# Candidate products of five of eight time stretches moved into the recurrences of a four-layer stack

## The chip, the cores and the metric

The kernel runs on one core of one Trainium2 chip. The metric is the time of one execution in microseconds (us), device time, as the median of several runs. Engines are named as in the profile: PE is TensorE (matmuls; PEld its weight loads), DVE is VectorE, ACT is ScalarE, POOL is GpSimd, SP the queue that issues the DMAs.

## The reference

32 rows of 256 time steps and 256 features go through four residual layers:

```
x = x + L0(cond, x)   # gated recurrence: z, r = sigmoid(x W + h U + cond C + b), hh = tanh(x W + (r*h) U + ..)
x = x + L1(cond, x)   # h = tanh(h*leak + sigmoid(h Wh + x Wz + b) * x)
x = x + L2(x, cond)   # f, i = sigmoid(x W_f + b_f), sigmoid(x W_i + b_i); s = f + i + eps
                      # new = i / s * (x W_h + b_h)               <- "candidate", weighed by i
                      # cumulative sum of log(f / s), exponentials, cumulative sum of scaled new, plus cond's part
x = x + L3(x, cond)   # per row two adapted 256x256 matrices: x + gelu(x M1) M2
```

L0 and L1 are recurrences over time, one step after the other; L2 and L3 are not.

## The kernel before, in words

The work has two stages.

**The recurrences.** One loop runs over t = 0 to 256; step t does step t of L0 and step t-1 of L1, with all 32 rows in one go, four quadrants of PE side by side. In each step the program order is: the products of r and z from the last h (`w_U_rz`, in the helper `product`, L606), the sigmoids, then whatever is due in this step (below), L1's product of its input (`w_l_Wz`), r*h (L760) turned to rhT, the product `w_U_h`, the kept part (1-z)h (L764), L1's product `w_l_Wh`, tanh (L690), the scan that makes h (L672, in two halves, inputs `other` and `keep`), its turn to hT (L682), the addition of x and hT on POOL (L787), and the next step's input product `w_W_rzh`. On POOL the residual addition of step t-3 (L722) comes first in a step, behind r*h by a dependency set by hand. Two of every four steps (t%4 = 0 or 3) open a new PSUM bank for L0 with four bf16 matmuls (L633), and every eighth step (t%8 = 2) opens one for L1, of 512 columns, after the input product.

Work of the later layers is laid beside the steps by dictionaries from step to calls (`transfers`, `products`, `moves`, `additions`, `sums`, `sigmoids`), filled by hand-written plans. Two jobs of the adaptation come first: the weights of L3 (16 of the steps 5 to 36 hold a matmul of it and POOL additions of 128x128, L467) and the matrices of L3 (32 steps to t = 227, whose sums with the base matrices, L522, run on DVE in five cuts). L2's gates for the first six of eight stretches of 32 time steps (NW_H = 6) take the steps that are left: a unit is one stretch, eight rows (q) and one of two feature halves (e). A product of a unit is two matmuls (k = 0, 1) of 128x256 into one half of the PSUM tile `pg`; one matmul goes into a step, whole (L93), or, in a few of the last steps, both go into one step in four quadrants each (L115). Then ACT's sigmoid (L130), on DVE the sum f+i (L135, reads two tiles in SBUF) and the guard (s times eps plus f, L138), and three stores to DRAM (L143).

**The last layers.** They work on eight groups of four rows. An order written out by hand, HEAD once and then TURN for turn = 2 to 9, says which piece of which group comes when; each word names a stage and a place, and the same order holds for every engine's own instructions. Here are the stages that matter: `in` fetches g, s and i of a group from DRAM; `lf` makes the gates of the last two stretches; `ls`, `lg` their sum and guard on DVE; `c` the candidate, W_h times x, two matmuls of 512 columns over all eight stretches (2 rows, one feature half), four of them a group; `m` (weigh, L875) adds the bias to it and multiplies it by i, on DVE from PSUM; `ln` and `exp` on ACT; `sum` (L897), `w` (L903), `new` (L915), `cum` (L920) and `h0` (L924) on DVE; `x` (L931) adds the hidden state to the rows on POOL, by a dependency behind the DVE piece that precedes it in the list; `mid` and `last` are the two products of L3 (L938), with gelu on ACT between; `y` (L960) is the final addition on DVE, from PSUM. Of the DVE pieces only m and y read PSUM; the others with two tensor inputs read both from SBUF.

Of the kernel before, what the change touches and what calls it, by code (L numbers as in the profile page):

```python
# [16 lines left out]
B = 32  # L17
T = 256
# [11 lines left out]
CB = 8  # L30
NH = T // CT
NW_H = 6
EPS = 1e-8


# [4 lines left out]
def kernel(ctx: ExitStack, tc: tile.TileContext, a, out: bass.AP):  # L40
# [26 lines left out]
    def vec(name, c):  # L67
        i = VECS.index(name)
        return vecs[:, i, c : c + 1]
# [21 lines left out]
    def gate_product(ps, w, e, k, rows, h0, h1):  # L91

        nc.tensor.matmul(  # L93
            ps[:, 0 : (h1 - h0) * (rows.stop - rows.start) * CT].rearrange(
                "p (h b t) -> p h b t", h=h1 - h0, t=CT
            ),
            w[:, k, e * P : (e + 1) * P],
            X2[:, k, rows, h0 * CT : h1 * CT].rearrange("p b (h t) -> p h b t", t=CT),
            start=(k == 0),
            stop=(k == NC - 1),  # L100
        )

    def gate_unit(h, q, e, banks):

        t = {}

        def multiply(name, w, k, by_quadrants):
            rows = slice(q * CB, (q + 1) * CB)
            if not by_quadrants:
                gate_product(banks[name], w, e, k, rows, h, h + 1)  # L110
                return

            for j in range(Q):
                js = slice(j * SQ, (j + 1) * SQ)
                nc.tensor.matmul(  # L115
                    banks[name][js].rearrange("p (b t) -> p b t", t=CT),
                    w[:, k, e * P + js.start : e * P + js.stop],
                    X2[:, k, rows, h * CT : (h + 1) * CT],
                    start=(k == 0),
                    stop=(k == NC - 1),  # L120
                    skip_group_check=True,
                    tile_position=(0, j * SQ),
                )

        def unit_tile(name):
            t[name] = gu.tile([P, CB * CT], FP, name=f"gate_{name}", tag=f"gate_{name}")
            return t[name]

        def sigmoid(name):
            nc.scalar.activation(  # L130
                unit_tile(name), banks[name], AF.Sigmoid, bias=vec("b_" + name, e)
            )

        def add_up():
            nc.vector.tensor_add(unit_tile("s"), t["f"], t["i"])  # L135

        def guard():
            nc.vector.scalar_tensor_tensor(  # L138
                unit_tile("g"), t["s"], EPS, t["f"], ALU.mult, ALU.add
            )  # L140

        def store(name):
            nc.sync.dma_start(out=waiting[q][:, "gsi".index(name), e, h], in_=t[name])  # L143

        return multiply, sigmoid, add_up, guard, store

    parts_f = {}

# [19 lines left out]
    gi = ctx.enter_context(tc.tile_pool(name="gates_in", bufs=1))  # L168
    gated = {}

    def fetch_chunk(g, i, e, hs=slice(0, NW_H)):
        name = "gsi"[i]
        if e == hs.start == 0:
            pool, bufs = (gp, 2) if i == 2 and g % 3 else (gi, 1)
            gated[name, g] = pool.tile(
                [P, NC, NH, GB * CT], FP, name=f"in_{name}", tag=f"in_{name}", bufs=bufs
            )
        q, half = divmod(g, CB // GB)
        cols = slice(half * GB * CT, (half + 1) * GB * CT)
        nc.sync.dma_start(out=gated[name, g][:, e, hs], in_=waiting[q][:, i, e, hs, cols])  # L180

    def fetch(g, i):
        for e in range(NC):
# [16 lines left out]
    with ExitStack() as rec:  # L200
# [43 lines left out]
        def at(when, t, f, *args):  # L244
            when.setdefault(t, []).append((f, args))
# [307 lines left out]

        free = [t for t in range(CT + 3, T) if t not in products]
        twice = range(T - 14, T - 4, 2)
        free = sorted(free + list(twice))
        stored = {}
        for h in range(NW_H):  # L560
            for q in range(B // CB):
                for e in range(NC):
                    while free[0] < (h + 1) * CT + 3:
                        free.pop(0)
                    multiply, sigmoid, add_up, guard, store = gate_unit(
                        h, q, e, {"f": pg[:, 0], "i": pg[:, 1]}
                    )
                    for name, w in (("f", w_f), ("i", w_i)):
                        ts, free[:NC] = free[:NC], []
                        for k, t in enumerate(ts):  # L570
                            by_quadrants = any(t in twice for t in ts)
                            at(products, t, multiply, name, w, k, by_quadrants)
                        at(sigmoids, t, sigmoid, name)
                    at(sums, t + 1, add_up)
                    at(sums, t + 2, guard)
                    for n, name in enumerate("isg"):
                        stored[q] = t + 2 + n // 2 + (n == 2)
                        at(transfers, stored[q], store, name)
        first_late = [
            first_late_gate(name, w, e, {"f": pg[:, 0], "i": pg[:, 1]})  # L580
            for e in range(NC) for name, w in (("f", w_f), ("i", w_i))
# [16 lines left out]
        def due(when, t):  # L598
            return [f(*args) for f, args in when.get(t, ())]

        def product(ps, cols, hT, w):


            for k in range(NC):
                for j in range(Q):
                    last = nc.tensor.matmul(  # L606
                        ps[j * B : (j + 1) * B, cols],
                        hT[:, k, :],
                        w[:, k, j, :],
                        start=False,  # L610
                        stop=False,
                        skip_group_check=True,
                        tile_position=(0, j * B),
                    )
            return last
# [93 lines left out]
        with tc.manual_schedule():  # L709
# [16 lines left out]
            for t in range(T + 1):  # L726
# [15 lines left out]
                    finish_1()  # L742
                    late = None
                due(moves, t)
                due(products, t)
                if t == T:
                    first_late[1][1]()
                if run1:
                    if s == 0:
                        begin_1(0, U1_0)  # L750
                    done = product(p_1[s], cols_1(s), by_chunk(pairs1[s][:, :, 0]), w_1z)
                    if run0:

                        after(done, z_done)
                rh_done = kept_done = None
                if run0 and t > 0:
                    rh = sp.tile([P, S], FP, name="rh", tag="rh")
                    for c in range(NC):
                        cs = bass.ts(c, B)
                        rh_done = nc.vector.tensor_mul(rh[:, cs], r[:, cs], h[:, cs])  # L760
                    rhT = turned("rhT", rh)
                    product(p_0[t], cols_0(t, 2, 2), rhT, w_uh)

                    kept_done = nc.vector.scalar_tensor_tensor(  # L764
                        kept, z, 1.0, h, ALU.subtract, ALU.mult, reverse0=True
                    )

                    after(kept_done, rz_done)
# [82 lines left out]
        )  # L851

    def late(g, name, e):
        return gated[name, g][:, e, LATE].rearrange("p h n -> p (h n)")

    def late_sum(g, e):
        return nc.vector.tensor_add(late(g, "s", e), parts_f[g, e], late(g, "i", e))
# [3 lines left out]
            late(g, "g", e), late(g, "s", e), EPS, parts_f.pop((g, e)), ALU.mult, ALU.add  # L861
        )

    def candidate(g, u):
        r, e = divmod(u, NC)
        b0 = g * GB + r * 2
        ps = pp.tile([P, 512], FP, name="ps_c", tag="ps_c")
        pcs[g, u] = ps.rearrange("p (h n) -> p h n", h=NH)
        for k in range(NC):
            gate_product(ps, w_n, e, k, slice(b0, b0 + 2), 0, NH)  # L870

    def weigh(g, u):
        r, e = divmod(u, NC)
        m = gated["i", g][:, e, :, r * 2 * CT : (r + 1) * 2 * CT]
        return nc.vector.scalar_tensor_tensor(  # L875
            m, pcs.pop((g, u)), vec("b_c", e), m, ALU.add, ALU.mult
        )

    def logs(g, q):
# [77 lines left out]
    def finish(g, b):  # L957
# [15 lines left out]
    }  # L973

    TURN = """
        lf:0 new:2 new:3 cum:2 sum:0.0 mid:1 in:2 mid:0 sum:1.0 cum:3 h0:2.0 lf:1 sum:0.1
        sum:3.1 last:1 sum:1.1 sum:3.0 w:1 exp:1 h0:3.1 h0:2.1 w:0 ls:0 h0:3.0 ls:1 c:0
        sum:2.0 w:3 lg:0 lg:1 x:2 m:0 y:1 x:3 exp:0 last:0 c:1 m:1 exp:3 c:3 y:0 mid:2 mid:3
        new:1 sum:2.1 new:0 w:2 cum:0 cum:1 c:2 h0:0.1 h0:0.0 exp:2 ln:1 h0:1.1 h0:1.0 ln:0
        last:2 x:1 m:3 last:3 y:2 in:1 x:0 m:2 in:0 y:3  # L980
    """

    HEAD = """
        in:2@2 lf:0@0 ls:0@0 lf:1@0 lg:0@0 c:2@0 c:1@0 ls:1@0 lg:1@0 ln:1@0 m:2@0 m:1@0
        sum:2.1@0 sum:2.0@0 c:0@0 ln:0@0 m:0@0 w:2@0 sum:3.1@0 sum:0.1@0 in:2@1 in:1@1
        sum:3.0@0 sum:0.0@0 sum:1.1@0 w:0@0 lf:0@1 lf:1@1 c:3@0 sum:1.0@0 ls:1@1 c:3@1 m:3@0
        exp:0@0 in:0@1 w:1@0 m:3@1 new:0@0 exp:1@0 lg:1@1 ls:0@1 new:1@0 w:3@0 exp:2@0
        cum:1@0 c:1@1 cum:0@0 h0:1.0@0 h0:0.0@0 exp:3@0 h0:1.1@0 lg:0@1 ln:1@1 x:1@0 ln:0@1
        c:2@1 m:1@1 c:0@1 h0:0.1@0 in:1@2 x:0@0 m:2@1 m:0@1 in:0@2
    """  # L990

    with tc.manual_schedule():
# [82 lines left out]
```

## Time and profile before

| what | us |
|---|---|
| time, median of 3 runs (950.96 to 952.18) | 951.61 |
| span of the profiled execution, first to last instruction | 950.9 |
| start, to the first h of the recurrence | about 15 |
| recurrences, steps 1 to 255 | 15 to 733 |
| last steps of L1 and start of the last layers | 733 to 739 |
| last layers | 739 to 951 |

For the profiled execution the span is what is given as its own time; the median of the timed runs lies 0.7 us above it, the shortest run 0.1. A row of the timeline gives start, duration, engine, line, operation, output<-input, shapes and a count; several instructions in a row are merged, and the duration is then from the first start to the last end. An fp32 matmul appears as two records. The time in brackets is how long the engine had been idle, and what ended that. The table of windows gives the busy time of each engine in a stretch, the granted clock of PE and the share of time in which the DMA engines were at work (1.00 and 0.73 are such shares).

### The profile page before, as it was taken

The numbers are of one execution on the slowest core, as the hardware profiler recorded it, in microseconds if no ns is written. First come the engines' busy times: TensorE is split into PE (matmuls) and PEld (weight loads), VectorE is DVE, ScalarE is ACT, GpSimd is POOL, SyncE is SP. The second block draws the span as 40 slices with busy tenths as digits, with TensorE's granted clock in tenths as the row PEclk, the third lists the DMA queues.
The fourth block names the chain that finished last, engine by engine and source line by source line (L and its number), as shares of the span: only waits on it lengthen the run. The fifth ranks groups of instructions, "written<-read, shape, count | busy, mean of one in ns | idle before, by whom it ended". The sixth has DMA issues, their size and how long they took to land.

```text
span 950.9 us, 55227 instructions
## 1 busy us (share of the span) xinstructions
PE 919.3 (97%) x22822; PEld 630.0 (66%) x22822; DVE 788.3 (83%) x3409; ACT 573.3 (60%) x2652; POOL 236.0 (25%) x594
## 2 busy tenths in 40 slices
PE   7999999999999999999999999999999799999978
PEld 4666666666666666666666666666676467777756
DVE  5777788888888888888888888888877899999995
ACT  3455555555555555555555555555555878889973
POOL 1233322222222222222222222222222012222222
PEclk9999999999999999999999999999999999999989
DMA  8345212222222222222222222341232457777643
GB/s 259 114 118 156 80 52 87 71 73 91 70 88 78 86 76 66 92 71 87 72 72 92 66 92 66 121 131 61 83 115 74 132 166 231 230 219 223 190 156 124
DMA packets 109726, 107.72 MB, mean 113 GB/s; under 512 B 9857, under 2 KB 96673, under 8 KB 109474
## 3 DMA queue, kind: packets, MB, share of 16 engines
q1 hardware_dynamic: 109474, 104.19, 35.2%
q8 instruction: 179, 2.93, 1.4%
q14 instruction: 73, 0.60, 0.2%
HBM read 59.06 MB, written 45.09 MB: 110 GB/s over the span
## 4 chain that ended last, share of the span: by engine, by line
PE 81%; DVE 11%; ACT 3%; issue 2%; DMA 1%; SPq 0%; POOL 0%; DVEq 0%; POOLq 0%; ACTq 0%
PE p L606 46%; PE ps_l L938 11%; PE pg L93 10%; PE ps_c L93 5%; DVE h L672 5%; PE p L633 3%; PE ps_g L93 2%; PE pw L510 2%; ACT other L690 2%; DVE hT L682 1%; ACT r L690 1%; DVE cc L897 1%; DMA w_W_rzh<-in_W_rzh_dram 1%; DVE rh L760 1%; DVE gate_g L138 1%
## 5 line engine op out<-in xcount | busy, mean ns | idle before, releaser
L606 PE MATMUL p<-w_W_rzh,xT 128*32 128x192 f32 x4096 | 213.8, 326 | 0.7 <-DMA w_W_rzh<-in_W_rzh_dram 0.7
L690 ACT ACTIVATE other<-p 128x32 f32<-128x32 f32 x512 | 74.3, 200 | 171.6 <-PE p L606 171.6
L672 DVE TENSOR_TENSOR_SCAN h<-other,keep 128x64 f32<-128x64 f32 x512 | 121.3, 279 | 66.3 <-ACT other L690 62.9
L606 PE MATMUL p<-w_U_rz,hT 128*32 128x128 f32 x4080 | 166.1, 279 | 6.4 <-issue 0.3
L787 POOL TENSOR_TENSOR pairs<-xT,hT 128x64 f32<-128x64 f32 x256 | 82.3, 322 | 327.1 <-DVE other L803 301.9
L690 ACT ACTIVATE r<-p 128x32 f32<-128x32 f32 x510 | 72.8, 195 | 149.9 <-PE p L606 149.9
L722 POOL TENSOR_TENSOR X<-pairs,h1T 128x64 f32<-128x64 f32 x256 | 102.7, 401 | 214.7 <-DVE rhT L682 211.1
L606 PEld LDWEIGHTS p<-w_U_rz,hT 128*32 128x32 f32 x4080 | 97.0, 108 | 85.8 <-DVE hT L682 83.7
L672 DVE TENSOR_TENSOR_SCAN pre<-other,pairs 128x128 f32<-128x128 f32 x256 | 123.4, 482 | 33.9 <-ACT pairs L794 0.2
L606 PEld LDWEIGHTS p<-w_W_rzh,xT 128*32 128x32 f32 x4096 | 124.4, 110 | 22.9 <-DMA w_W_rzh<-in_W_rzh_dram 1.4
L606 PEld LDWEIGHTS p<-w_l_Wz,pairs 128*32 128x32 f32 x4096 | 78.2, 110 | 84.7 <-issue 69.3
L794 ACT ACTIVATE pairs<-h1T,leak 128x32 f32<-128x32 f32 x510 | 133.6, 314 | 0.4
L606 PE MATMUL p<-w_l_Wz,pairs 128*32 128x64 f32 x4096 | 119.2, 225 | 3.5 <-ACT keep L740 0.9
L606 PE MATMUL p<-w_U_h,rhT 128*32 128x64 f32 x4080 | 106.2, 221 | 0.0
L606 PE MATMUL p<-w_l_Wh,h1T 128*32 128x64 f32 x4080 | 104.1, 219 | 0.0
L760 DVE TENSOR_TENSOR rh<-r,h 128x32 f32<-128x32 f32 x510 | 75.0, 189 | 32.2 <-ACT r L690 6.2
L682 DVE STREAM_TRANSPOSE hT<-h 128x32 f32<-128x32 f32 x512 | 84.2, 198 | 0.0
L931 POOL TENSOR_TENSOR X<-X,w 128x512 f32<-128x512 f32 x32 | 41.0, 1291 | 162.3 <-DVE in_g L860 99.5
L682 DVE STREAM_TRANSPOSE rhT<-rh 128x32 f32<-128x32 f32 x510 | 80.0, 195 | 0.0
L606 PEld LDWEIGHTS p<-w_l_Wh,h1T 128*32 128x32 f32 x4080 | 76.2, 110 | 0.1
L606 PEld LDWEIGHTS p<-w_U_h,rhT 128*32 128x32 f32 x4080 | 69.6, 108 | 5.0
L719 ACT ACTIVATE h1T<-pre 128x64 f32<-128x64 f32 x256 | 69.7, 272 | 1.1 <-DVE pre L672 1.1
(110 smaller groups left out, 1472.7 us busy)
## 6 DMA issues: line engine op xcount, KB each, us to landing
adapted<-wm SPq DMA_DIRECT2D x128, 128.0 KB
wt<-adapted SPq DMA_DIRECT2D x28, 512.0 KB
w<-in_W_dram SPq DMA_DIRECT2D x32, 256.0 KB
out_dram<-y SPq DMA_DIRECT2D x32, 256.0 KB
xT<-in_xT_dram SPq DMA_DIRECT2D x60, 128.0 KB
gates<-gate_i SPq DMA_DIRECT2D x48, 128.0 KB
gates<-gate_s SPq DMA_DIRECT2D x48, 128.0 KB
gates<-gate_g SPq DMA_DIRECT2D x48, 128.0 KB
```

What stands on the lines that cost most here:

```text
L93: nc.tensor.matmul(ps[:, 0 : (h1 - h0) * (rows.stop - rows.start) * CT].rearrange("p (h b t) -> p h b t", h=h1 - h0, t=CT), w[:, k, e * P ...
L606: last = nc.tensor.matmul(ps[j * B : (j + 1) * B, cols], hT[:, k, :], w[:, k, j, :], start=False, stop=False, skip_group_check=True, tile_ ...
L672: nc.vector.tensor_tensor_scan(*(x[:, ns].rearrange("p n u -> p (n u)") for x in (done, other, pairs)), 0.0, ALU.mult, ALU.add,)
L682: nc.vector.transpose(dst[:, c], src[:, bass.ts(c, B)])
L690: nc.scalar.activation(dst[:, bass.ts(c, B)], src[:, bass.ts(c, B)], function)
L719: nc.scalar.activation(flat(h1T), pre, AF.Tanh)
L722: return nc.gpsimd.tensor_add(X2[:, :, :, s], by_chunk(pairs1.pop(s)[:, :, 0]), h1s.pop(s))
L760: rh_done = nc.vector.tensor_mul(rh[:, cs], r[:, cs], h[:, cs])
L787: nc.gpsimd.tensor_add(by_chunk(pairs1[t][:, :, 0]), x_of(t), hT)
L794: nc.scalar.activation(by_chunk(pairs1[s][:, :, 1])[:, c], h1T[:, c], AF.Copy, scale=leak[:, c : c + 1],)
L931: after(nc.gpsimd.tensor_add(x, x, ws[g][:, b]), on_vector)
L938: nc.tensor.matmul(ps[:, e, :], matrices[row][:, m, k, e * P : (e + 1) * P], src[:, k, :], start=(k == 0), stop=(k == NC - 1),)
```

## The change

The change makes the candidate of the first five stretches (NC_H = 5) in the recurrences too. A unit there now has three products, f, i and c, for h < 5, and two for h = 5: 136 instead of 96, each of two matmuls. The products take the two halves of `pg` in turn. Where there are not enough free steps a step is "doubled": both matmuls go into it, by quadrants, and then L1's `w_l_Wz` is issued behind `w_U_h` instead of ahead of it, and the wait for z, which its last matmul took early, goes to the last quadrant matmul. 84 of the 188 steps that hold gate products are doubled. The sum f+i moves from DVE to POOL, with no dependency of its own behind other work of the step. A new DVE piece, `weigh_unit`, multiplies the candidate with i, in place, one step after its product, and the store of i follows that; the guard goes to a step that holds no weighing. The fetch of group 0 begins three steps later (t = 243 instead of 240), since the last store of its rows comes at t = 241 instead of 238.

In the last layers the candidate is left with three stretches: it now goes by four rows and 384 columns, two a group instead of four, and so does the weighing. HEAD and TURN are new. In TURN four `x` pieces stand as `h0:2.0 ls:0 x:2 new:3 sum:0.0`, `h0:3.1 exp:1 x:3 new:0 y:0 ls:1`, `h0:0.1 x:0 new:1 lg:0 w:2` and `h0:1.1 x:1 y:2 .. m:1 .. m:0 y:3` (other engines' pieces left out); before they stood as `lg:1 x:2 m:0 y:1 x:3 m:1 y:0` and `x:1 m:3 y:2 x:0 m:2 y:3`.

```diff
+NC_H = 5
...
-            nc.vector.tensor_add(unit_tile("s"), t["f"], t["i"])
+            nc.gpsimd.tensor_add(unit_tile("s"), t["f"], t["i"])
...
+        def weigh_unit(bank):
+            nc.vector.scalar_tensor_tensor(
+                t["i"], bank, vec("b_c", e), t["i"], ALU.add, ALU.mult
+            )
...
+        banks = pg[:, 0], pg[:, 1]
+        begins = {t for t in range(T) if t % 4 in (0, 3)}
+        free = [t for t in range(CT + 3, T - 1) if t not in products]
+        wanted = [
+            (h, q, e, name) for h in range(NW_H) for q in range(B // CB) for e in range(NC)
+            for name in ("f", "i", "c")[: 3 if h < NC_H else 2]
+        ]
...
+            while free[0] < max((h + 1) * CT + 3, last_read[n % 2]):
+                free.pop(0)
+            short = NC * (len(wanted) - n) - len(free)
+            now = free.pop(0)
+            if short > 0 and (now not in begins or short > sum(t not in begins for t in free)):
+                doubled.add(now)
+            for k in range(NC):
+                if k and now not in doubled:
+                    now = free.pop(0)
+                at(products, now, multiply, bank, w, k, now in doubled)
+            if name == "c":
+                at(sums, now + 1, weigh_unit, bank)
+                busy.add(now + 1)
+                last_read[n % 2] = now + 2
+                at(transfers, now + 2, store, "i")
...
+            at(sums, t + 1, add_up)
+            t += 2
+            while t in busy:
+                t += 1
+            busy.add(t)
+            at(sums, t, guard)
...
-                due(products, t)
+                multiplied = due(products, t)
...
-                    done = product(p_1[s], cols_1(s), by_chunk(pairs1[s][:, :, 0]), w_1z)
-                    if run0:
-
-                        after(done, z_done)
+                    if t in doubled:
+                        after(multiplied[-1], z_done)
+                    else:
+                        done = product(p_1[s], cols_1(s), by_chunk(pairs1[s][:, :, 0]), w_1z)
+                        if run0:
+
+                            after(done, z_done)
...
                     product(p_0[t], cols_0(t, 2, 2), rhT, w_uh)
+                    if t in doubled:
+                        product(p_1[s], cols_1(s), by_chunk(pairs1[s][:, :, 0]), w_1z)
...
+    def candidate(g, e):
         ps = pp.tile([P, 512], FP, name="ps_c", tag="ps_c")
...
+            gate_product(ps, w_n, e, k, slice(g * GB, (g + 1) * GB), NC_H, NH)
...
     TURN = """
+        new:2 lf:0 sum:3.1 lf:1 sum:2.0 mid:0 sum:3.0 cum:2 sum:1.0 c:1 sum:1.1 h0:2.1 h0:2.0
+        ls:0 x:2 new:3 sum:0.0 sum:0.1 cum:3 w:0 mid:1 h0:3.0 exp:0 w:1 h0:3.1 exp:1 x:3 last:0
+        last:1 new:0 mid:2 y:0 ls:1 cum:0 lg:1 sum:2.1 y:1 h0:0.0 in:2 h0:0.1 x:0 new:1 mid:3
+        lg:0 w:2 last:2 cum:1 w:3 exp:2 h0:1.0 last:3 ln:1 h0:1.1 x:1 y:2 ln:0 in:1 exp:3 m:1
+        c:0 m:0 y:3 in:0
     """
```

## The prediction

> **What bounds the kernel now.** I read the page first: TensorE (PE) is busy nearly all the span, VectorE (DVE) 83% of it, GpSimd (POOL) a quarter.
>
> ```profile
> PE 919.3 (97%) x22822; PEld 630.0 (66%) x22822; DVE 788.3 (83%) x3409; ACT 573.3 (60%) x2652; POOL 236.0 (25%) x594
> ```
>
> Such shares mix two stages. The timeline of the recurrences (to about 736 us) shows a fixed rhythm: `w_U_rz` starts at 665.32, 668.12, 670.92, so 2.80 us a step. Steps with a gate product keep that rhythm, and so do the few without one: the step is a chain (hT, `w_U_rz`, sigmoid, rh, turn, `w_U_h`, tanh, the h scan, turn), and the product lies in a gap of PE. What counts here is whether anything reaches the chain. One step, with the places that the change touches:
>
> ```profile
> 663.90 0.40 POOL L722 TENSOR_TENSOR X<-pairs,h1T 128x64 f32<-128x64 f32 x1 [0.82 <-DVE rhT L682]
> ...
> 664.03 0.36 DVE L522 TENSOR_TENSOR wm<-pw,w_base_upT 128x204 f32<-128x204 f32 x1
> ...
> 664.30 0.41 DVE L135 TENSOR_TENSOR gate_s<-gate_f,gate_i 128x256 f32<-128x256 f32 x1
> ...
> 664.69 0.48 DVE L672 TENSOR_TENSOR_SCAN h<-other,keep 128x64 f32<-128x64 f32 x2
> ```
>
> The sum f+i (L135) sits just ahead of the h scan and ends as it starts: no delay. POOL is free from 664.30 until hT is there.
>
> In the last layers I read the busy time of four turns of the list, each 24.35 us; one of them (columns: us, PE, PEld, DVE, ACT, POOL, clock, DMA share, GB/s):
>
> ```profile
> 824.56:848.91 24.35, 24.35 (x98) 18.10 (x97) 23.76 (x41) 21.75 (x32) 5.12 (x5) 1.00 0.73 226
> ```
>
> PE is full, DVE 0.6 us short of it. The change takes work from both, so DVE bounds next, and the third view asks what else holds DVE up. At the tail two POOL adds (L931) meet DVE:
>
> ```profile
> 921.47 1.29 DVE L960 TENSOR_TENSOR y<-ps_l,X 128x512 f32<-128x512 f32 x2
> ...
> 921.71 2.94 POOL L931 TENSOR_TENSOR X<-X,w 128x512 f32<-128x512 f32 x2 [11.36 <-DVE w L903]
> ...
> 922.67 0.85 DVE L915 TENSOR_TENSOR w<-in_i,w 128x512 f32<-128x512 f32 x1
> ...
> 923.44 1.75 DVE L897 TENSOR_TENSOR_SCAN cc<-f,s 128x256 f32<-128x256 f32 x1
> ```
>
> y, with one input in PSUM, runs beside POOL at its usual 0.69 each. L915, with two inputs in SBUF, takes 0.85 instead of 0.68; L897, also two, takes 1.75 instead of 0.67 and ends 0.54 after POOL does. POOL's pair takes 2.94 instead of 2.50: its second add stood still until L915 was through, then ran ahead of the scan. The same elsewhere: L924 at 759.48 takes 1.13 instead of 0.47 beside an L931, and L135 takes 0.55 (697.70) when L722 is still running, ending 0.28 after it. L522, L875 and L960, which read PSUM, never lengthen. So POOL and a DVE operation with two SBUF inputs exclude each other, and POOL goes next in turn. The old list puts its L931s beside y and m.
>
> **The change, part by part.** Times are against the profiled span, 950.9; the median of the runs is 951.61, 0.7 more.
>
> (1) *f+i moves to POOL, 48 times.* On POOL 128x128 (L467) takes 0.45 and 128x512 (L931) 1.28, so 128x256 by a straight line takes 0.73. It stands behind L722 in POOL's order, so it runs from about 664.27 to 665.00 of the step shown. The h scan has two SBUF inputs (other, keep) and starts at 664.69. A blocked scan ends its streaming after POOL: 0.28 after it for 128 columns (L672 pre beside L787), so about 0.145 for the 64 of one half. The first half then ends at 665.15 instead of 664.97: 0.17 on the chain (0.15 to 0.20 by where the add begins). 48 x 0.17 = **+8.2**. Bounds: nothing if the scan isn't held; 48 x 0.3 = 14.4 if it restarts whole. I take 0.17, since three kinds of DVE rows show that shape. Queued behind the add on POOL is L787, which waits for hT anyway, and behind L787 the next step's `w_l_Wz`. That the add also waits for the store of an older f+i is no news: L135 did too.
>
> (2) *40 candidate products (80 matmuls) join 96 gate products; 84 steps now hold both matmuls of a product, by quadrants.* In the old plan five such steps took 2.887, because `w_l_Wz` stood ahead of `w_U_h`. The new one puts it behind `w_U_h`, so rhT is met in time, but its 16 records, 0.225 from first to next (675.17 to 675.40 for their like), now stand ahead of the next `w_U_rz`. The wait for z goes from `w_l_Wz` to the last quadrant matmul; behind it waits `w_U_h`, which needs rhT 0.3 later anyway. What room is there? Here is a step that opens a new bank for layer 1 (t%8 = 2):
>
> ```profile
> 673.48 0.40 PE L633 MATMUL p<-parts,eye 128*32 128x512 bf16 x4
> ...
> 673.72 0.64 PE L606 MATMUL p<-w_U_rz,hT 128*32 128x128 f32 x16
> ```
>
> The 512 columns stream for about 0.21, to 673.69: room 0.03. Where layer 0's bank is opened (t%4 = 0 or 3), the last `w_W_rzh` matmul leaves about 0.06; in the others, without that 0.16, 0.22 to 0.24. I counted the plan: of 84 double steps 27 have t%8 = 2, 9 have t%4 = 0 or 3, 48 neither. 27 x 0.19 + 9 x 0.16 = 6.6. Nine of these 36 also carry a sum, whose delay gives PE the room: less 9 x 0.16 = 1.4. **+5.1**. The 48 others cost nothing, hidden by 0.22; if that is short by 0.05 they cost 2.4. Bounds: 0, if the modelled ends are late, to 36 x 0.225 + 2.4 = 10.5. The five old late steps go: **-0.4**.
>
> (3) *weigh* (128x256, one input in PSUM) takes the place on DVE that f+i leaves: L875 at 512 columns takes 0.745, less 256 columns at 1.04 ns = 0.48, against 0.41: at most 0.03 late in the 29 steps that also hold an L522, **+0.2**. The store of i follows it instead of the sigmoid; count and size of the stores stay, and SP's queue is idle for 2 us and more between issues there (701 to 733), which hides them; without that a late store would hold only the fetches at the start of the last layers. ACT's sigmoids are the same 96.
>
> (4) *Last layers, one turn.* PE loses 16 records of 0.43 and gains 8 of 0.32: 24.35 - 6.9 + 2.6 = 20.05. ACT has five table loads where it had six (1.28 each): 20.5. DVE loses 4 x 0.66 (L875, start to start) and gains 2 x 0.53: the rest sums to 20.9 by start-to-start rows, with 0.1 that I can't place: 22.05. So DVE would set a turn of 22.05, were there no POOL. But the new list sets x:2 ahead of new:3, sum:0.0; x:0 ahead of new:1, lg:0; x:3 ahead of new:0, y:0, ls:1; only x:1 lies beside y:2, m:1, m:0. By the tail rows each L931 lets one DVE operation through, then holds the next for 1.1 to 1.2: x:2 1.15, x:0 1.15, x:3 0.55 (y:0 fills half), x:1 0. Sum 2.85, turn **24.9**: 0.55 more than now. The fetches stay behind ln as now and land a few us later, ln of the next group 20 us later. The waits of DVE don't hide the 2.85: exp:0 ends 0.4 ahead of new:0, ln and exp:3 by two and more.
>
> (5) *Head and end.* DVE's head starts at 739.4 and sums start at 743.8, as now (ACT's table load and logarithms come first); then 14.1 of DVE work instead of 17.6, and the 2.2 and 1.0 waited for candidates go: new:2 at 758.4 instead of 764.1, -5.7. Turn 2 pays for x:0 and x:1 of group 0 as well, +2.2 + 0.55; turns 3 to 7 +0.55 each, 2.75; turn 8 (22.9 now; 24.9 - 2.4 without m, ls, lg) -0.4; the last turn, rows one by one instead of in pairs, 12.9 instead of 14.5, -1.6. Together **-2.2**. Bounds: 22.05 a turn gives -25; 1.2 for every x gives +6.
>
> Sum: 8.2 + 5.1 - 0.4 + 0.2 - 2.2 = +10.9: span 961.8, median run **962.5**.
>
> **Rivals.** *A, faster:* an L931 doesn't overtake a queued DVE operation but waits for the next that reads PSUM. Place: the last layers; price: the 2.85 a turn. Then turns are 22.05 (6 x -2.3), the head keeps its 5.7, turn 8 saves 3.2, the end 2.6: -25, and with +13 ahead of it 939. It decides once x costs under 1.2 a turn. For it: L960 runs beside every L931 now. Against: the scan at 923.44, overtaken. 0.20. *B, no price in the recurrences:* the add is done early enough and PE's modelled ends are late: 951.6 - 2.2 = 949.5. For it: halves of L467 beside the scan cost nothing. Against: those end at 47.23, the scan starts at 47.21; this add ends 0.3 later. 0.12. *C, a cold PE:* PE idles 4.9 us a turn, most of it ahead of mid:3, which waits for x:3. After 4.45 us of idleness at 759.62 a 512-column record took 0.85 instead of 0.43, for about 4 us; after 1.48 us (737.52) nothing happened. If each turn pays 2.4 for it and y waits: 6 x 2.4 = 14, 976. Against: last:2 has some 3 us to y:2. 0.10.
>
> [...]
>
> **The numbers.** My forecast 0.58, A 0.20, B 0.12, C 0.10. Forecast alone: 954 to 970, by its bounds. The range 941 to 974 leaves out half of A and half of C. What measurement can tell from no change is 0.2%, 1.9 us: faster 0.24 (A and a third of B), same 0.08, slower 0.68.
>
> **What would show it.** Right: in steps with a POOL sum the h scan takes 0.17 longer and the step 2.97; double steps at t%8 = 2 last 2.99, other double steps 2.80; in a turn, L897, L860 or L903 lengthen to 1.7 beside L931, and the turn is 24.9. Wrong: steps of 2.80 throughout, or turns near 22. A later last hT than 733 + 13 means a part of (1) or (2) is too small.

## The result, and the profile after

The changed kernel takes 968.64 us (median of 4 runs, 967.94 to 969.12) where the kernel before takes 951.89 in the same session: a ratio of 1.0172, with a 95% interval of 1.0156 to 1.0188. It is slower by 16.7 us; 10.9 had been forecast. The profiled execution spans 967.3 us, 16.4 more than before. The last h of the recurrences ends at 754.05 instead of 733.18, so the recurrences are 20.9 longer; the rest takes 213.3 instead of 217.7, 4.4 less.

Line numbers after the change: L606 (`product`) is now L638, L672 (scans) L704, L690 (tanh) and its like L722, L722 (residual) L754, L135 (f+i) L134, L897 (sum) L931, L903 (w) L937, L915 (new) L949, L920 (cum) L954, L924 (h0) L958, L931 (x) L965, L938 (products of L3) L972, L960 (y) L994; `ls` is L894 and `lg` L897 now, and L714 the turn (L682). The busy times:

```profile
PE 916.9 (95%) x23830; PEld 661.3 (68%) x23830; DVE 795.6 (82%) x3385; ACT 572.7 (59%) x2646; POOL 295.3 (31%) x642
```

PE has 1008 matmul records more and is yet 2.4 us less busy; POOL is busy 59 us more. DVE is busy 7 us more; a DVE operation that waits for POOL counts as busy (an L937 of 1.71 us below, where 0.68 is usual).

**A step with a sum.** Timeline of one step of the recurrences after the change (start, duration, engine, line, operation):

```profile
548.52 0.40 POOL L754 TENSOR_TENSOR X<-pairs,h1T 128x64 f32<-128x64 f32 x1 [0.84 <-DVE rhT L714]
...
548.88 0.72 POOL L134 TENSOR_TENSOR gate_s<-gate_f,gate_i 128x256 f32<-128x256 f32 x1
549.08 0.29 ACT L722 ACTIVATE other<-p 128x32 f32<-128x32 f32 x2 [0.68 <-PE p L638]
549.31 0.62 DVE L704 TENSOR_TENSOR_SCAN h<-other,keep 128x64 f32<-128x64 f32 x2 [0.58 <-ACT other L722]
```

The scan of h starts on time and takes 0.62 where it took 0.48; POOL's add runs until 549.60, into it. Over the trace a step of this kind lasts 2.955 (median of the six that have no doubled step beside them), a plain one 2.798: 0.156 more.

**A doubled step without a sum.** The same view, some 90 us earlier:

```profile
456.69 0.65 PE L638 MATMUL p<-w_U_rz,hT 128*32 128x128 f32 x16
...
457.33 1.15 PE L115 MATMUL pg<-X,w_W_i 128*32 128x256 f32 x16
...
457.58 0.24 ACT L772 ACTIVATE keep<-p 128x64 f32<-128x64 f32 x1
...
457.86 0.31 DVE L714 STREAM_TRANSPOSE rhT<-rh 128x32 f32<-128x32 f32 x2
...
458.22 0.43 PE L638 MATMUL p<-w_U_h,rhT 128*32 128x64 f32 x15
...
458.49 0.22 PE L638 MATMUL p<-w_U_h,rhT 128*32 128x64 f32 x1
...
458.75 0.29 ACT L722 ACTIVATE other<-p 128x32 f32<-128x32 f32 x2 [0.79 <-PE p L638]
```

From `w_U_rz` to tanh it is 2.06 here (456.69 to 458.75); in the step with the sum, which is not doubled, it was 1.94 (547.14 to 549.08). There `w_U_h` began 1.47 after `w_U_rz` and its sixteen records started within 0.19 (its row: 548.61, 0.41 long, the last record 0.22); here it begins at 1.53 (458.22), 0.22 after the last product record of the first quadrant (458.00), which is the pace at which that quadrant's records had started (457.33, 457.57, 457.79, 458.00), and the last record, in the quadrant whose matmuls waited for z (`keep`, to 457.82), starts 0.27 after the first. rhT is ready 1.48 after `w_U_rz` (at 458.17), as in plain steps, so the lateness arises behind it. From the end of one h to the end of the next, the median of the 59 doubled steps without a sum is 2.92: each is 0.12 late in itself, at any place of the eight-step pattern.

**A turn in the last layers.** DVE and POOL at x:0:

```profile
847.33 3.61 POOL L965 TENSOR_TENSOR X<-X,w 128x512 f32<-128x512 f32 x1 [3.85 <-DVE w L958]
```

```profile
847.11 0.68 DVE L949 TENSOR_TENSOR w<-in_i,w 128x512 f32<-128x512 f32 x1
847.72 0.41 DVE L897 SCALAR_TENSOR_TENSOR in_g<-in_s,gate_f 128x256 f32<-128x256 f32 x1
848.05 0.68 DVE L937 TENSOR_TENSOR w<-cc,s 128x512 f32<-128x512 f32 x1
848.65 1.21 DVE L954 TENSOR_TENSOR_SCAN w<-anew,w 128x512 f32<-128x512 f32 x1
849.79 1.71 DVE L937 TENSOR_TENSOR w<-cc,s 128x512 f32<-128x512 f32 x1
```

x:0 needs 1.28 alone and stands for 3.61: L949, under way, and three more (L897, L937, L954) run at their usual lengths, and only the fifth, L937, is held, for 1.03. The turn is 24.45 (x:0 to x:0, 847.33 to 871.79), and in it DVE has no gap while PE does (row of the table of windows):

```profile
850.00:875.00 25.00, 22.52 (x92) 18.05 (x91) 25.00 (x39) 21.01 (x31) 9.33 (x6) 0.93 0.74 230
```

### The profile page after: what moved, and what is told of

The parts are those of the page before. It is cut to its first block, busy times and chain, and to the rows that moved or that the text cites. A ratio compares the mean times of both kernels' runs of the same rounds, so it can differ in the third digit from the quotient of the medians.

```text
span 967.3 us, 57349 instructions
## 1 busy us (share of the span) xinstructions
PE 916.9 (95%) x23830; PEld 661.3 (68%) x23830; DVE 795.6 (82%) x3385; ACT 572.7 (59%) x2646; POOL 295.3 (31%) x642
## 3 DMA queue, kind: packets, MB, share of 16 engines
q8 instruction: 186, 3.05, 1.3%
## 4 chain that ended last, share of the span: by engine, by line
PE 74%; DVE 16%; ACT 4%; issue 3%; DMA 2%; POOL 0%; SPq 0%; POOLq 0%; DVEq 0%; ACTq 0%
PE p L638 49%; PE pg L115 9%; PE pg L94 7%; DVE cc L931 4%; PE p L665 3%; DVE h L704 2%; PE ps_l L972 2%; PE pw L517 2%; DVE w L958 1%; DVE w L949 1%; DVE w L954 1%; DVE w L937 1%; DVE y L994 1%; ACT other L722 1%; DMA in_i<-gates 1%
## 5 line engine op out<-in xcount | busy, mean ns | idle before, releaser
L638 PE MATMUL p<-w_W_rzh,xT 128*32 128x192 f32 x4096 | 226.6, 326 | 0.0
L704 DVE TENSOR_TENSOR_SCAN h<-other,keep 128x64 f32<-128x64 f32 x512 | 125.5, 286 | 78.7 <-ACT other L722 76.9
L722 ACT ACTIVATE other<-p 128x32 f32<-128x32 f32 x512 | 74.6, 199 | 182.2 <-PE p L638 182.2
L638 PE MATMUL p<-w_U_rz,hT 128*32 128x128 f32 x4080 | 169.5, 278 | 4.4 <-DVE hT L714 1.4
L754 POOL TENSOR_TENSOR X<-pairs,h1T 128x64 f32<-128x64 f32 x256 | 102.7, 401 | 221.7 <-DVE rhT L714 214.5
L722 ACT ACTIVATE r<-p 128x32 f32<-128x32 f32 x510 | 72.8, 195 | 138.8 <-PE p L638 134.9
L704 DVE TENSOR_TENSOR_SCAN pre<-other,pairs 128x128 f32<-128x128 f32 x256 | 123.3, 482 | 35.3 <-POOL pairs L824 1.3
L638 PEld LDWEIGHTS p<-w_W_rzh,xT 128*32 128x32 f32 x4096 | 135.6, 110 | 21.7 <-issue 2.1
L638 PEld LDWEIGHTS p<-w_U_rz,hT 128*32 128x32 f32 x4080 | 104.1, 108 | 67.1 <-DVE hT L714 65.1
L638 PE MATMUL p<-w_l_Wz,pairs 128*32 128x64 f32 x4096 | 127.8, 223 | 3.9 <-ACT keep L772 1.6
L638 PEld LDWEIGHTS p<-w_l_Wz,pairs 128*32 128x32 f32 x4096 | 89.7, 110 | 58.3 <-issue 45.6
L638 PE MATMUL p<-w_U_h,rhT 128*32 128x64 f32 x4080 | 118.7, 221 | 0.1
L638 PE MATMUL p<-w_l_Wh,h1T 128*32 128x64 f32 x4080 | 116.2, 219 | 0.7 <-issue 0.7
L965 POOL TENSOR_TENSOR X<-X,w 128x512 f32<-128x512 f32 x32 | 67.4, 2108 | 131.9 <-DVE w L958 94.6
L638 PEld LDWEIGHTS p<-w_U_h,rhT 128*32 128x32 f32 x4080 | 83.0, 108 | 14.8 <-DVE keep L801 0.3
L638 PEld LDWEIGHTS p<-w_l_Wh,h1T 128*32 128x32 f32 x4080 | 87.5, 110 | 1.2 <-issue 0.9
L714 DVE STREAM_TRANSPOSE hT<-h 128x32 f32<-128x32 f32 x512 | 84.1, 199 | 0.0
L972 PE MATMUL ps_l<-mid,wt 128*128 128x256 f32 x256 | 66.7, 419 | 14.9 <-ACT mid L985 14.9
L714 DVE STREAM_TRANSPOSE rhT<-rh 128x32 f32<-128x32 f32 x510 | 80.2, 195 | 0.0
```

The lines of the kernel that those rows point to most:

```text
L638: last = nc.tensor.matmul(ps[j * B : (j + 1) * B, cols], hT[:, k, :], w[:, k, j, :], start=False, stop=False, skip_group_check=True, tile_ ...
L704: nc.vector.tensor_tensor_scan(*(x[:, ns].rearrange("p n u -> p (n u)") for x in (done, other, pairs)), 0.0, ALU.mult, ALU.add,)
L714: nc.vector.transpose(dst[:, c], src[:, bass.ts(c, B)])
L722: nc.scalar.activation(dst[:, bass.ts(c, B)], src[:, bass.ts(c, B)], function)
L754: return nc.gpsimd.tensor_add(X2[:, :, :, s], by_chunk(pairs1.pop(s)[:, :, 0]), h1s.pop(s))
L965: after(nc.gpsimd.tensor_add(x, x, ws[g][:, b]), on_vector)
```

## The experiments

My theory after this: (a) the add on POOL holds the h scan; (b) a doubled step is late by its own quadrant matmuls and the wait for z on the last of them, and, where a bank is opened, makes the next step late by `w_l_Wz`; (c) DVE bounds the turn, and the new list puts `x` where it holds DVE up. The main rival for (a) and (b): the extra work on PE and DVE costs, wherever it stands. For (c): the clock, 0.93 in the row above, where PE idles 2.5 of 25 us.

A ratio is always to the kernel before, timed again in the same session, for its own median moved from session to session (951.89, 954.39, 952.24, 953.93 us). So runs are compared by their ratios; a difference of two of them is uncertain by about 0.003, some 3 us. Positions such as the last h come from one profiled execution of each run.

**f+i back on DVE.**

```diff
-            nc.gpsimd.tensor_add(unit_tile("s"), t["f"], t["i"])
+            nc.vector.tensor_add(unit_tile("s"), t["f"], t["i"])
```

> One part undone: the sum f+i is back on DVE, all else as in the changed kernel (968.6). Theory (the sum on POOL holds up the h scan, because both read two tiles in SBUF): in steps with a sum that are not doubled the 0.156 us go (23 of them), in doubled ones only about 0.04, because those are 0.117 late already and the end of the POOL sum hides that: -4.5 in all, 964. If the two prices add up without overlap: 48 x 0.156 = -7.5, 961. Rival (the new steps are late because DVE and PE are crowded, and where the sum runs doesn't matter): no change or slower, since DVE gets 0.41 us more in 48 steps: 968 to 972.

Measured: ratio 1.0131 (1.0107 to 1.0156), 0.0041 under the changed kernel, or 3.9 us. Its timeline at the same step:

```profile
547.23 0.56 DVE L134 TENSOR_TENSOR gate_s<-gate_f,gate_i 128x256 f32<-128x256 f32 x1
547.67 0.29 ACT L722 ACTIVATE other<-p 128x32 f32<-128x32 f32 x2 [0.68 <-PE p L638]
547.90 0.47 DVE L704 TENSOR_TENSOR_SCAN h<-other,keep 128x64 f32<-128x64 f32 x2
```

The sum now pays for its meeting with L754 (0.56 instead of 0.42) and still ends before the scan, which takes 0.47. Steps with a sum go from 2.955 to 2.808, doubled steps with a sum only from 2.958 to 2.919. So the two delays of one step don't add: the add on POOL ends at a fixed time, and a scan that is late by 0.12 anyway finds it 0.04 from done. 23 single steps x 0.147 + 25 doubled x 0.04 = 4.4. In the profiled execution itself the last h came just 1.2 earlier; other steps were longer there, of which more below. So the step lengths show the mechanism, and the total is less sure than 3.9 sounds: the two other pairs of runs below that differ in this edit alone give 2.0 and 5.5.

**The wait for z moved behind `w_U_h`.**

```diff
                     if t in doubled:
-                        after(multiplied[-1], z_done)
-                    else:
+                    if t not in doubled:
...
-                        product(p_1[s], cols_1(s), by_chunk(pairs1[s][:, :, 0]), w_1z)
+                        done = product(p_1[s], cols_1(s), by_chunk(pairs1[s][:, :, 0]), w_1z)
+                        after(done, z_done)
```

> One part undone: in the doubled steps the early wait for z goes back from the last quadrant matmul to the last matmul of w_l_Wz, which in those steps stands behind w_U_h; the sum stays on POOL. Theory (the last quadrant's matmul starts only after z, runs 0.46 us after that, and w_U_h of that quadrant begins late): doubled steps without a sum go from 2.917 to about 2.80, those with one stay at 2.956, the steps after a doubled step stay late: 59 x 0.117 = -6.9, 962. Rival (the four quadrants simply have too much to stream ahead of w_U_h, wait or not): w_U_h begins 0.08 late instead of 0.12, -2 at most, 966.5.

Measured: ratio 1.0274 (1.0246 to 1.0301), slower than the changed kernel; the last h at 767.25. My expectation fell. The doubled step itself did go down, from 2.917 to 2.880: 0.037 of its lateness is the wait for z, and the other 0.08 is there without it: the quadrants' own streaming. One such step of this run:

```profile
460.46 0.64 PE L638 MATMUL p<-w_U_rz,hT 128*32 128x128 f32 x16
461.10 1.07 PE L115 MATMUL pg<-X,w_W_i 128*32 128x256 f32 x16
461.98 0.43 PE L638 MATMUL p<-w_U_h,rhT 128*32 128x64 f32 x16
```

`w_U_h` begins 1.52 after `w_U_rz`, with nothing ahead of it but the product; in plain steps of this run it begins at 1.45. But steps of all kinds became longer at odd places. Waits of PE, first in this run, then in the changed kernel:

```profile
PE p L638 <- issue: 6.7, 17, 1.0
```

```profile
PE p L638 <- issue: 1.5, 2, 0.7
```

17 times PE stood in the middle of a product with nothing to wait for that the profile shows. One of them, in this run:

```profile
462.43 0.22 PE L638 MATMUL p<-w_l_Wh,h1T 128*32 128x64 f32 x1
463.11 0.37 PE L638 MATMUL p<-w_l_Wh,h1T 128*32 128x64 f32 x12 [0.46 <-issue]
```

I counted PE's instructions (weight loads, matmuls, semaphore waits) up to each such gap. Of the gaps over 0.2 us in the recurrences, 31 lie at instruction 192 or 193 after a multiple of 256, and these sum to 15.2 us; in the changed kernel it is 5 such gaps and 1.9 us. The page of the changed kernel has a DMA queue that fits (packets, MB, share):

```profile
q8 instruction: 186, 3.05, 1.3%
```

3.05 MB in 186 packets is 16.4 KB each; over 2 x 23830 PE instructions it is 64 bytes each, so one packet holds 256 instructions, an estimate from this row and PE's. By the DMA records the instruction after such a gap comes 1.40 us (median) after the last of these packets has landed, and no boundary is crossed sooner than 1.1 after that; the boundaries without a gap are crossed 2.1 us after it in the changed kernel, about 1.8 in this run. So PE ran out of instructions, as far as position and time can show it. The difference, 13.3 us, is as much as the 13.2 by which the last h is later, though the doubled steps, 59 x 0.037 = 2.2 shorter, should have left only 11; those 2 us I can't place. Why the fetches come later with this order (they begin 1.13 us after the previous boundary instead of 0.90, medians) I did not find out.

**Both of these.** The two edits above in one kernel.

> The two edits together: sum on DVE and the wait for z behind w_U_h. Theory: the prices overlapped in 25 doubled steps, so that together they give more than the sum of the two: -4.5 - 6.9 - 25 x 0.117 = -14.3, 954.5; what is left of the recurrences' loss is the steps after a doubled one at t%8 = 2 or at an opening (27 x 0.19 + 9 x 0.10 = 6.0). Rival (independent prices): -11.4, 957; rival (neither matters): 968.

Measured: ratio 1.0216 (1.0192 to 1.024), last h at 759.49, with 11.8 us of the same gaps. The theory's 954.5 was far off, again for the gaps. Against the run with the wait moved alone, f+i on DVE is worth 0.0058 here, or 5.5 us, of which 3.4 are the gaps that this run has less. That the gaps come back in another kernel with the same order, at the same place modulo 256, speaks against a chance of one execution.

**`w_l_Wz` ahead of `w_U_h` in doubled steps too.**

```diff
                     if t in doubled:
-                        after(multiplied[-1], z_done)
-                    else:
-                        done = product(p_1[s], cols_1(s), by_chunk(pairs1[s][:, :, 0]), w_1z)
...
+                    done = product(p_1[s], cols_1(s), by_chunk(pairs1[s][:, :, 0]), w_1z)
+                    if run0:
+                        after(done, z_done)
...
-                    if t in doubled:
-                        product(p_1[s], cols_1(s), by_chunk(pairs1[s][:, :, 0]), w_1z)
```

> The changed kernel, but in the 84 doubled steps w_l_Wz stands ahead of w_U_h again (with the wait for z on its last matmul), as in every other step and as in the late doubled steps of the kernel before. Theory (the 0.117 of a doubled step has two parts: the product's 16 quadrant matmuls stream past the time at which w_U_h is due, and their last part waits for z; the lateness of the step after comes from w_l_Wz standing ahead of the next w_U_rz): doubled steps take 2.887, as the five late ones of the kernel before did, which is 0.03 less than in the changed kernel; the step after a t%8 = 2 falls from 2.99 to 2.82 and w_U_rz starts 0.16 after the end of h again, not 0.236. 84 x 0.03 + 27 x 0.17 + 9 x 0.08 = 7.8 less, last end of h at 746. Rival (w_l_Wz adds its own 0.22 of streaming ahead of w_U_h, which the product's streaming has made late already): doubled steps at 3.05 to 3.1, 84 x 0.15 = 12.6 more, less the 5 of the steps after: last end of h at 761. A second thing is looked at: the time that weight loads of L638 wait for 'issue', 48.8 us in the changed kernel and 60.9 in the run with the wait for z moved behind.

Measured: ratio 1.0118 (1.0092 to 1.0145), 5.1 us better than the changed kernel; last h at 749.69. Doubled steps without a sum take 2.886, the step after one at t%8 = 2 takes 2.801, and `w_U_rz` starts 0.158 after h instead of 0.236: all three as the theory had it. The total is 4.4 and not 7.8, because gaps at the instruction boundaries are 4.9 us here instead of 1.9, and because doubled steps that carry a sum stay at 2.958. The weight loads' wait for "issue" is 52.2 us, between the 48.8 and 60.9 of the two other runs. The timeline of a doubled step in this run shows the new order:

```profile
455.59 1.05 PE L115 MATMUL pg<-X,w_W_i 128*32 128x256 f32 x16
...
456.45 0.41 PE L638 MATMUL p<-w_l_Wz,pairs 128*32 128x64 f32 x16
...
456.68 0.41 PE L638 MATMUL p<-w_U_h,rhT 128*32 128x64 f32 x16
```

`w_l_Wz` ahead of `w_U_h` costs 0.006 against the order that has neither it nor the wait ahead (2.886 to 2.880), less than the wait for z on a quadrant (0.037), and nothing in the next step. The order that the change chose was the dearer one.

**The old lists for the last layers**, with the words of the candidate that no longer exist (c:2, c:3, m:2, m:3) left out of HEAD and TURN; the recurrences are the changed ones.

> The changed recurrences with the old HEAD and TURN, from which only c:2, c:3, m:2 and m:3 are taken out (the work is the same as in the changed kernel, the order is the old one; x stands beside y and m again). Theory (three of four x additions hold DVE up by 2.6 us a turn in the new list): here x:2 and x:3 lie beside m:0 y:1 m:1 y:0, and x:1, x:0 beside only two y, so about 1.3 a turn is held up: turns of 23.3 instead of 24.45, 6 turns, about -6: 962.5; the h scans and steps as in the changed kernel. Rival (POOL's additions are not what sets the turn, the new order gains elsewhere, by one table load less on ACT and by its head): slower than the changed kernel, 970 or more.

Measured: ratio 1.0134 (1.0104 to 1.0164); the last layers take 207.6 instead of 213.3, 5.7 less. The ratio gives only 3.6 us of that: in this execution the same recurrences were 2.4 longer (last h at 756.50). The turn is 23.44 (POOL, x:2 of one turn to the next, 842.97 to 866.41). POOL at the pair x:1 and x:0, and DVE at both pairs:

```profile
851.77 2.97 POOL L965 TENSOR_TENSOR X<-X,w 128x512 f32<-128x512 f32 x2 [6.29 <-DVE w L958]
```

```profile
845.07 0.97 DVE L949 TENSOR_TENSOR w<-in_i,w 128x512 f32<-128x512 f32 x1
...
852.76 2.53 DVE L949 TENSOR_TENSOR w<-in_i,w 128x512 f32<-128x512 f32 x2
```

Two L949 take 2.53 instead of 1.28, and one 0.97 instead of 0.66: held 1.56 a turn, where the new list has 2.58 (1.03 at L937, about 1.07 at two L931, 0.48 at L894). The difference of 1.02 is the difference of the turns, 1.01. The rival, 970 or more, falls.

**y:1 beside x:0**, one word of the new list moved.

```diff
-        last:1 new:0 mid:2 y:0 ls:1 cum:0 lg:1 sum:2.1 y:1 h0:0.0 in:2 h0:0.1 x:0 new:1 mid:3
+        last:1 new:0 mid:2 y:0 ls:1 cum:0 lg:1 sum:2.1 h0:0.0 in:2 h0:0.1 x:0 y:1 new:1 mid:3
```

> The changed kernel with one word of TURN moved: y:1 stands behind x:0 instead of ahead of h0:0.0, so that VectorE's next work after x:0 becomes ready reads PSUM. Theory (a POOL add of two SBUF inputs can start only when VectorE's next operation doesn't read two SBUF inputs or a scan has just ended; x:0 lets four operations pass now, and stops the fifth): x:0 falls from 3.60 to 1.3 to 1.7, the w (L937) that it stopped from 1.71 to 0.68, and some 0.6 of that comes back at the operation behind y. The turn falls from 24.45 to 24.0, seven turns 2 to 4 us. Rival (POOL gets in after a fixed wait or by chance): x:0 stays over 2.5 and the turn where it is. Rival two (the turn is not VectorE's): x:0 shorter, the turn unchanged.

Measured: x:0 falls from 3.61 to 1.27 and L937 from 1.71 to 0.66, and L949 is held instead:

```profile
848.44 1.27 POOL L965 TENSOR_TENSOR X<-X,w 128x512 f32<-128x512 f32 x1 [3.25 <-DVE w L958]
```

```profile
848.22 0.68 DVE L994 TENSOR_TENSOR y<-ps_l,X 128x512 f32<-128x512 f32 x1
848.82 1.44 DVE L949 TENSOR_TENSOR w<-in_i,w 128x512 f32<-128x512 f32 x1
```

The turn is 24.16, and the last layers take 211.2 (967.5 less 756.3), 2.1 less: the low end of what was expected. The ratio, 1.0166 (1.0146 to 1.0186), can't be told from the changed kernel's; in this execution the recurrences were 2.3 longer, with 4.8 us of gaps at instruction boundaries instead of 1.9. The run also settles the clock. A row of its windows, with the same turn of 24.16 in it:

```profile
800.00:825.00 25.00, 21.54 (x93) 16.86 (x92) 25.00 (x40) 21.19 (x30) 7.18 (x6) 1.00 0.75 233
```

The granted clock is 1.00 here and 0.93 in the next window of the same run, and the turn (POOL, x:1 at 805.45, 829.62 and 853.78) does not change. DVE has no gap in either window (25.00 of 25.00), and there the lower clock of PE costs nothing.

The two held operations end a like time after POOL's add: L937 of 1.71 ends 0.56 after it in the changed kernel, L949 of 1.44 ends 0.55 after it here, and both take 0.66 to 0.68 where they are not held. Which of the two starts next when both wait is another matter: one, two or four DVE operations went ahead of a waiting add in the changed kernel (x:3, x:2, x:0).

**f+i on DVE and the old lists.**

> The changed kernel with f+i back on VectorE and with the old lists for the last layers. Theory (the two costs are independent: 3.9 us by the run with f+i on VectorE, 3.7 by the run with the old lists): 968.6 - 7.6 = 961, that is 1.009 to 1.010 of the kernel before. Rival (the old lists gained only because the recurrences ended on a different step for the lists): under 5 us together, 1.012 or more.

Measured: ratio 1.0113 (1.0093 to 1.0132), between the theory and the rival; the two savings alone come to 0.0079, together they are 0.0059. Against the old lists alone, f+i on DVE is worth 0.0021 here, 2.0 us. The last layers have all of theirs (207.2 us); the last h came at 753.17, no sooner than with f+i on DVE alone.

**All three places mended**: f+i on DVE, `w_l_Wz` ahead, the old lists.

> The run before with w_l_Wz ahead of w_U_h in the doubled steps as well: all three places undone where the changed kernel loses, with its 40 products and their weighing still beside the recurrences. Theory: last end of h at 733.2 + 84 x 0.087 = 740.5, last layers 207.6 as with the old lists, span 948.1, ratio 0.997 (0.994 to 1.000), faster than the kernel before. Rival (w_l_Wz's streaming adds to the product's): last end of h 755 or later, ratio 1.013 or more.

Measured: ratio 1.0008 (0.9991 to 1.0024). Last h at 743.42, 3 us later than expected; last layers 208.3. So undoing the change in these three places takes away the loss, 0.0164 of 0.0172, and the main rival falls: nearly the same work, placed otherwise, costs nothing that can be measured. It isn't free where it stands: the recurrences are still 10.2 longer than before the change, 84 x 0.087 = 7.3 of it the doubled steps, and the last layers gain 9.4.

**How many products are worth moving.** The same kernel once more, and with four and six stretches of the candidate in the recurrences.

```diff
-NC_H = 5
+NC_H = 4
```

> The same kernel as the last of the runs before (f+i on VectorE, w_l_Wz ahead of w_U_h in doubled steps, old lists), measured again beside the two that follow: 84 doubled steps, ratio 1.001 (0.999 to 1.003).

> The same with the candidate's products of four stretches of eight made beside the recurrences, not five (NC_H = 4): 68 doubled steps, 512 columns a candidate in the last layers. Theory (with the three faults mended a product costs about what it saves): recurrences 16 x 0.087 = 1.4 shorter; in the last layers a weighing of 512 columns takes 0.746 (before) against 0.605, two a turn, eight turns: 2.3 longer. Together +0.9 against the run above, within 0.2%. Rival one (the products themselves are dear, by the instruction fetch or PE's load): 3 us or more faster than the run above. Rival two (the last layers gain from every product): 3 us or more slower.

> The same with six stretches of eight (NC_H = 6): 100 doubled steps, 256 columns a candidate in the last layers. Theory: the opposite, -0.9 against the run with five, within 0.2%. Rival one: 3 us or more slower. Rival two: 3 us or more faster, and then faster than the kernel before.

Measured: five 0.9997 (0.9981 to 1.0014), four 0.9983 (0.9972 to 0.9994), six 1.0053 (1.0032 to 1.0075). Four against five can't be told: the two intervals overlap. Six is 5.3 us slower than five, not 0.9 faster: the last h is 4.7 later (746.99, 742.25), of which the 16 more doubled steps explain 1.4, and the last layers take 210.4 instead of 208.0. That is the size which the first rival forecast for six; for four, where it forecast 3 us or more to be gained, it is 1.3. POOL's rows show where the last layers lose: every other turn is now 24.5. Two rows of the table of windows; the first holds the gaps of a longer turn:

```profile
800.00:825.00 25.00, 21.26 (x90) 17.72 (x90) 23.12 (x40) 21.63 (x31) 5.08 (x5) 0.93 0.74 221
825.00:850.00 25.00, 21.68 (x98) 17.94 (x96) 25.00 (x41) 23.87 (x34) 5.54 (x5) 1.00 0.78 236
```

DVE does have gaps there: y waits 1.03 for a product of PE (820.28) and a sum 0.84 for a logarithm on ACT (824.44), and the granted clock is 0.93. Whether the clock makes these waits or the order of the list does, no run tells. Of the other 3.3 us of the recurrences some 2 are more gaps at instruction boundaries. With four stretches the turn is 23.45 as with five, though its two weighings are 0.13 longer each: the `new` behind them (L949 of the changed kernel) are held less (mean 0.946 for 0.992, four a turn), as I read it because more of x lies beside operations that read PSUM. Four stretches are the best that I have, 0.17% under the kernel before: the interval just leaves out 1, but it is less than the 0.2% that I had called a difference.

## Why the prediction was right, and where its sizes were off

The direction, the place and the order of the losses held: the recurrences lose, the last layers gain little because `x` holds DVE. The total came nearer than its parts: the recurrences were under-sized by 7.8 and the gain of the last layers by 2.2, and these errors partly cancel. By the steps:

- **(1), f+i on POOL.** Mechanism and size of one step are right: the add takes 0.73 (median 0.730), the scan is held by 0.156 (0.17 predicted). The sum of +8.2 is too high: 25 of the 48 adds are in doubled steps, where the two delays overlap. Taking the add away gave 3.9 by the ratios, 4.4 by the step lengths.
- **(2), doubled steps.** The 0.19 at t%8 = 2 is there, in the step behind the doubled one (2.99), and there is none at plain places; after an opening of layer 0's bank it was 0.10 instead of 0.16. The step that failed is "The 48 others cost nothing", with its reason, that behind the wait for z "waits `w_U_h`, which needs rhT 0.3 later anyway". I looked at the room ahead of the next `w_U_rz` and not at the room ahead of `w_U_h` in the same step. There is none: the quadrant matmuls stream past the time at which `w_U_h` is due (0.08), and the z on the last of them adds 0.037. The old plan had shown it: its doubled steps took 2.887, but I put that down to `w_l_Wz` standing ahead of `w_U_h`, and without `w_l_Wz` there they still take 2.880. 59 doubled steps without a sum x 0.117 = 6.9, which is most of the 7.8 by which the recurrences were under-sized (13.1 predicted, 20.9 measured). Counting by kinds gives 23 x 0.156 + 25 x 0.158 + 59 x 0.117 + 27 x 0.19 + 9 x 0.10 = 20.5. The relief by a sum's delay, 9 x 0.16 in the prediction, was small: behind a doubled step at t%8 = 2 that carries a sum the next step still takes 2.95.
- **(3), weigh.** L142 takes 0.480 (mean of 40), the 0.48 predicted. The 1.04 ns a column in it is near what two rows of the kernel before give: 0.41 for the 256 columns of L135 and 0.68 for the 512 of L915, 1.05 ns a column.
- **(4), the turn.** 24.45 for 24.9. The holds sum to 2.58, for 2.85. The rule behind them, "each L931 lets one DVE operation through", is wrong: it was one, two and four (x:3, x:2, x:0). It mattered little, since the hold that follows is near 1.05 at x:0 and x:2 alike, and 0.48 at x:3, where y fills half.
- **(5), head and end.** Turn 2 began 5.9 earlier against the last h (5.7 predicted). The last layers gained 4.4, for 2.2: the shorter turn makes most of that.
- **Rivals.** A falls: turns are not 22.05, and `x` does get in ahead of operations that read SBUF. B falls by the step lengths. C had its condition, a granted clock under 1 (0.93 in 850:875), but not its price: with y:1 moved the turn is 24.16 at 1.00 and at 0.93 alike, and DVE has no gap in either window.

That the new list costs more than the old one would, which the places of x in (4) suggest but the prediction did not price, was shown by putting the old one back: 5.7 us of the last layers, 3.6 by the ratios.

## What to carry to other kernels

Work that fits a gap of an engine by its busy time must also end before the next link of the chain wants that engine; read both edges, the one in the same step and the one in the next. Two delays in one step, each of which ends at a time of its own, need not add (here 0.156 and 0.117 alone, 0.158 together). A hand-written order that places POOL adds beside the VectorE operations that read PSUM is worth keeping when the work around it is thinned out (here 5.7 us of the last layers), and the adds lose their cover if just those operations are the ones removed (here DVE was held 2.58 us a turn with the new list, 1.56 with the old).

## What the hardware showed that I had not expected

- PE seems to have run out of instructions: the packets of the instruction queue are 16.4 KB each, 256 instructions by the estimate above. At some of the boundaries PE stood for 0.2 to 1 us, reported as a wait for "issue"; the instruction after such a gap came 1.40 us (median) after the last packet had landed, while boundaries without a gap were crossed 2.1 us after it in the changed kernel, about 1.8 in the run with the most gaps. The gaps sum to 1.6 us in the kernel before, 1.9 in the changed one, 15.2 and 11.8 in the two with the wait for z behind `w_U_h`. Two executions with the same recurrences had 1.9 and 4.8, and their last h differed by 2.3. I saw it by position and by the DMA records and did not try to provoke it; the cause of the later fetches stays open.
- A POOL add that waits for VectorE got in after one, two or four of its operations (1.66, 2.18 and 3.60 us for an add of 1.28). Beside an operation that reads PSUM it ran at once (1.27, y:1 behind x:0); two of the others got in at the end of a scan, but in the old list one got in between two L949. I have no rule for it.
